# A message-passing network on one core: each tile's sums wait for the landing of a later piece's gather, and go tile by tile

## The chip, the cores and the metric

The kernel runs on one NeuronCore of a Trainium2 chip. The metric is the device time of one execution in microseconds (us); lower is better. Engines are named as in the profile: PE is TensorE (matmuls; PEld its weight loads), DVE is VectorE, ACT is ScalarE, POOL is GpSimd, which here issues the indirect DMAs, and SP is SyncE, which issues the plain ones.

## The reference

Four layers in a row act on x, 6250 nodes of 256 numbers; each is added to x after a layer normalisation. Cut to what matters here:

```
x = x + gat(layernorm(x), src, dst)            # layer 0: attention over 206250 edges, 4 heads of 64
x = x + moe(layernorm(x))                      # 8 experts, top 2
x = x + ngcf(layernorm(x), src, dst, weight)   # layer 1: weighted sums over the same 206250 edges
x = x + routed(layernorm(x), edge_index)       # 131072 more edges make the routing; 4 experts, top 2
```

The first is, for every node n and head, a softmax over the edges that end in n, and with it a sum over rows h[src]; the third is `segment_sum(weight * e[src], dst)`, then two dense products, a leaky ReLU and a division by the row's norm. Edges of the first and third come sorted by their target (`dst`); those of the fourth are sorted on the chip.

## The kernel before

An edge tile is 128 edges of the sorted list, and a piece is 8 tiles (`Q = 8`). A block is 128 nodes; there are 49. Because the edges are sorted, the tiles that can hold edges of block b form a window (`Stream.window`, L930), with a slack of 1024 edges on either side in the long lists and of 640 in the third. For one tile POOL gathers the 128 source rows from a table in DRAM by one indirect DMA; DVE makes a one-hot matrix for each block that the tile can touch (`one_hots`, L1056); and PE multiplies the one-hot matrix with the gathered rows into the block's accumulator in PSUM (the sums). An f32 matmul shows as two records, two passes, in the profile.

There are three such streams. The first two are the long ones: 1612 tiles, 202 pieces. Their order is written out by hand, within `tc.manual_schedule()`: every engine does its instructions in the order of the program text, and waits by semaphores for its operands and for its buffers.

*The first stream*, `gat_stream` (L1081) with `parts=1`, goes in steps. Step `s_` has:

- the gathers of piece `s_` (L1139) into one of 9 buffers; SP's loads for piece `s_ + 2`;
- for piece k = `s_ - 2`: the node products on PE (`node_parts`, L1160), the scores on DVE (`scores`, L1169 to L1175), and DVE's turned one-hots for the next piece (L1149);
- for piece q = `s_ - 7`: the sums of its tiles 0 and 1 (`sums(q, 0)`, L1239);
- in every fourth step a batch of 32 tiles: transposes on PE (`turn_scores`, L1185), two scans on DVE (`greatest`, L1191 to L1197);
- the one-hots for piece q + 1 (L1065); the sums of tiles 2 to 7 of piece q (`sums(q, 1)`); in a batch step the transposes back and the exponentials (`turn_back`, L1202 to L1210);
- the results of the blocks whose window has ended (`done`, L1650 to L1663), and DVE's product of messages for piece q + 1 (`messages`, L1217).

In a piece the sums go block by block, and within a block tile by tile.

*The second stream* (L1755 to L1795) has 6 buffers. Step `s_` gathers piece `s_` (L232, called in a helper), sums piece q = `s_ - 3` (L1780), does for ended blocks one stage each of a chain of functions (`side`, `dense`, `norm`, `next_ln`, `next_h`, `next_rows`; transposes on PE with copies on ACT, dense products, normalisations, and stores of the next layer's tables), and for piece k = `s_ - 2` scales the gathered rows by the edge weights on ACT (L1792) and makes the one-hots. A block's chain starts in the step after its last sum.

*The third stream* is `gat_stream` again with `parts=3`: the messages are split into three bf16 parts (L1222, L1224) and 787 tiles are summed by bf16 matmuls. Here `beside()` stands between the steps' parts: each call starts one unit of the last layer's feed-forward work, `inner` (L1533, four f32 passes of 512 columns) or `outer` (L1544, eight passes of 256), and finishes the unit before it by a gelu on ACT (L1538) or an addition on DVE (L1549).

Of the kernel before, what the change touches and what calls it, by code (L numbers as in the profile page):

```python
# [69 lines left out]
def tile_kernel(ctx, tc, src_ins, out):  # L70
    nc = tc.nc
# [157 lines left out]
        return v  # L229

    def gather(dst, table, si, t):
        nc.gpsimd.indirect_dma_start(  # L232
            out=dst, out_offset=None, in_=table,
            in_offset=bass.IndirectOffsetOnAxis(ap=si[:, t:t + 1], axis=0))


    def rstd_of(pool, var, n):
# [843 lines left out]
    def gat_stream(s, H, CD, si, il, dl, tab, NI, nid, early, done, parts=1, beside=None):  # L1081
# [6 lines left out]
        DH = H * CD  # L1088
# [3 lines left out]
        npiece = -(-T // Q)  # L1092
        PB = B // Q
        nbatch = -(-npiece // PB)
        with ExitStack() as st:
# [5 lines left out]
            with tc.tile_pool(name="split", bufs=1) as sp:  # L1101
                r = sp.tile([P, NT, ND], F32, name="r")
# [4 lines left out]
                nc.vector.tensor_copy(NB[:, :, 2, :], r)  # L1107
            ips = place_iota(pp)
            piece, Z, acc, turned, hots, dbs, kfs, ps, ended = {}, {}, {}, {}, {}, {}, {}, {}, []
            items, split = {}, {}  # L1110
            beside = beside or (lambda: False)

            def span(q):
                return q * Q, min(Q, T - q * Q)
# [10 lines left out]
            def load(q):  # L1125
                t0, n = span(q)
                dbs[q] = mp.tile([P, Q * P], I16, name="db", bufs=3)
                nc.sync.dma_start(dbs[q][:, :n * P], s.d16[t0 * P:(t0 + n) * P][None, :].to_broadcast([P, n * P]))
                if q % PB == 0:
                    i = q // PB  # L1130
                    kfs[i] = mp.tile([P, 3 * P + 1], BF, name="kf", bufs=3)
                    nc.sync.dma_start(kfs[i], bass.AP(tensor=s.keep.tensor, offset=s.keep.offset + i * B * P,
                                                      ap=[[P, B], [0, H], [1, 3 * P + 1]]))

            def gathers(q):
                t0, n = span(q)
                g = piece[q] = mp.tile([P, Q, W], F32, name="g", bufs=9)
                for j in range(n):
                    nc.gpsimd.indirect_dma_start(  # L1139
                        out=g[:, j, :DH + H], out_offset=None, in_=tab,  # L1140
                        in_offset=bass.IndirectOffsetOnAxis(ap=si[:, t0 + j:t0 + j + 1], axis=0))

            def turned_hots(q):
                t0, n = span(q)
# [83 lines left out]
            def sums(q, part):  # L1228
                t0, n = span(q)
                g = split[q]  # L1230
                for b, a, m, oh in hots[q]:
                    if b not in acc:
                        acc[b] = pp.tile([P, parts, W], F32, name="acc", bufs=2)
                        items[b] = early(b, mp)
                    lo, hi = s.window(b)
                    for t in range(a, a + m):
                        if (t - t0 < 2) == (part == 0):
                            m_ = g[:, t - t0, :] if parts == 1 else g[:, t - t0].rearrange("p s w -> p (s w)")
                            nc.tensor.matmul(acc[b].rearrange("p s w -> p (s w)"), oh[:, t - a], m_,  # L1239
                                             start=(t == lo), stop=(t == hi))  # L1240
                            if t == hi:
                                ended.append(b)
                if part == 1:
                    hots.pop(q)
                    split.pop(q, None)


            with tc.manual_schedule():
                load(0)
                load(1)  # L1250
                turned_hots(0)
                for s_ in range(max(npiece + 7, PB * nbatch + 3) + 1):
                    if s_ < npiece:
                        gathers(s_)
                    if s_ + 2 < npiece:
# [12 lines left out]
                    if batch:  # L1268
                        zt = turn_scores(i)
                        d, M = greatest(i, zt)  # L1270
                    if 0 <= q + 1 < npiece:
                        hots[q + 1] = one_hots(s, q + 1, mp, ips, dl, 4, F32 if parts == 1 else BF)
                    beside()
                    if 0 <= q < npiece:
                        sums(q, 1)
                    if batch:
                        turn_back(i, d, M)
                    beside()
                    while ended:
                        b = ended.pop(0)  # L1280
                        done(b, acc.pop(b), items.pop(b), mp)
                    if 0 <= q + 1 < npiece:
                        messages(q + 1)
                    beside()
                while beside():
                    pass
# [287 lines left out]
    def fast(flag_s0, last_d, dl_d):  # L1574
        s0 = flag_s0
# [102 lines left out]
        tab_e = dram.tile([NP, D], F32, name="tab_ef")  # L1678
# [3 lines left out]
        with tc.tile_pool(name="n1f", bufs=1) as ep, tc.tile_pool(name="n1fw", bufs=2) as mp, \  # L1682
# [14 lines left out]
                nc.sync.dma_start(tab_e[t0 * P:(t0 + n) * P].rearrange("(t p) d -> p t d", p=P), em[:, :n])  # L1697
            wg = layer1_weights(ep)
            ips = place_iota(pp)
            acc, piece, hots, ems = {}, {}, {}, {}  # L1700
            T = s0.T
            npiece = -(-T // Q)
            stages = {}

            def span(q):
                return q * Q, min(Q, T - q * Q)
# [50 lines left out]
            chain = {side: dense, dense: norm, norm: next_ln, next_ln: next_h, next_h: next_rows}  # L1757


            with tc.manual_schedule():  # L1760
                after = {}
                s_ = 0
                while s_ < npiece + 3 or any(k >= s_ for k in after):
                    if s_ < npiece:
                        t0, n = span(s_)
                        g = piece[s_] = mp.tile([P, Q, D], F32, name="g1", bufs=6)
                        for j in range(n):
                            gather(g[:, j, :], tab_e, si, t0 + j)
                    q = s_ - 3
                    if 0 <= q < npiece:  # L1770
                        t0, n = span(q)
                        g = piece.pop(q)
                        for b, a, m, oh in hots.pop(q):
                            lo, hi = s0.window(b)
                            if b not in acc:
                                acc[b] = pp.tile([P, D], F32, name="acc1", bufs=3)
                                ems[b] = mp.tile([P, D], F32, name="emb", bufs=3)
                                nc.sync.dma_start(ems[b], tab_e[b * P:(b + 1) * P])
                            for t in range(a, a + m):
                                nc.tensor.matmul(acc[b], oh[:, t - a], g[:, t - t0, :], start=(t == lo), stop=(t == hi))  # L1780
                            if hi == a + m - 1:
                                after.setdefault(s_ + 1, []).append((side, b, ()))
                    for f, b, args in after.pop(s_, []):
                        r = f(b, *args)
                        r = () if r is None else r if isinstance(r, tuple) else (r,)
                        if f in chain:
                            after.setdefault(s_ + 1, []).append((chain[f], b, r))
                    k = s_ - 2
                    if 0 <= k < npiece:
                        t0, n = span(k)  # L1790
                        for j in range(n):
                            nc.scalar.activation(piece[k][:, j, :], piece[k][:, j, :], AF.Copy,  # L1792
                                                 scale=wt[:, t0 + j:t0 + j + 1])
                        hots[k] = one_hots(s0, k, mp, ips, dl, 4)
                    s_ += 1  # L1795
# [19 lines left out]
    s0 = Stream("s0", I["src"].shape[0], SLACK0, N)  # L1815
# [32 lines left out]
```

## Time and profile before

| | |
|---|---|
| median of 3 runs | 6783.41 us (6782.30 to 6785.78) |
| the profiled execution | 6782.63 us, span of its instructions 6780.7 us |
| PE, DVE, ACT, POOL busy in the span | 5038.5, 3283.5, 1591.6, 4077.3 us |
| mean granted clock of PE | 0.845 |
| first stream, first to last gather's start | 183.0 to 2219.5 us (with the last one's end) |
| second stream | 3420.9 to 5437 us |
| third stream | 5457.2 to 6596 us |

The span is cut into 40 equal slices, and each digit is the busy share of a slice in tenths; PEclk is the clock that the throttle granted, in tenths of full speed:

```profile
PE   4477777777777669999577787877787727778778
PEld 3355555555555558888445555555555514445445
DVE  4466666666666781443422222222222246666663
ACT  2000000000000112322134444444444402222222
POOL 0677777777777012232167777777777767666650
PEclk9688888888888679999768888888888858889889
```

The two long stretches in which POOL stands at 7 are the first and the second stream; between them, where PE stands at 9, lies the mixture of experts. A busy POOL of 7 is the share of time in which a gather is being issued; what lies between two gathers is not counted.

### The profile page before, as it was taken

How to read it: one execution, taken by the hardware profiler on the slowest of the kernel's cores; microseconds unless marked ns; L12 is line 12 of the kernel's file. 1: busy time of each engine (PE TensorE's matmuls, PEld its weight loads, DVE VectorE, ACT ScalarE, POOL GpSimd, SP SyncE). 2: the span in 40 equal slices, each digit the busy share in tenths (PEclk: the TensorE clock that was granted, in tenths of full speed). 3: DMA queues.
4: the chain of work that ended last, by engine and by line, in shares of the span. 5: the costliest groups of instructions: out<-in, count | busy, mean ns of one | idle time of the engine just before them, and what ended most of it. 6: DMA issues, size and time to landing. Idle time of an engine off the chain costs nothing. (4 is left out here: it accounts for less than half of the span.)

```text
span 6780.7 us, 69471 instructions
## 1 busy us (share of the span) xinstructions
PE 5038.5 (74%) x23031; PEld 3781.3 (56%) x23031; DVE 3283.5 (48%) x7594; ACT 1591.6 (23%) x3641; POOL 4077.3 (60%) x4346
## 2 busy tenths in 40 slices
PE   4477777777777669999577787877787727778778
PEld 3355555555555558888445555555555514445445
DVE  4466666666666781443422222222222246666663
ACT  2000000000000112322134444444444402222222
POOL 0677777777777012232167777777777767666650
PEclk9688888888888679999768888888888858889889
DMA  4455555444555135557444343444433332222220
GB/s 138 137 138 138 139 136 138 137 138 135 140 138 136 46 107 194 181 190 237 144 121 112 112 113 111 113 113 112 112 112 112 112 84 42 43 44 37 42 42 12
DMA packets 462756, 777.63 MB, mean 115 GB/s; under 512 B 125744, under 2 KB 286928, under 8 KB 462355
## 3 DMA queue, kind: packets, MB, share of 16 engines
q0 software_dynamic: 190688, 461.74, 25.5%
q1 hardware_dynamic: 259166, 300.20, 14.6%
q10 hardware_dynamic: 12532, 11.16, 0.5%
q8 instruction: 185, 3.03, 0.2%
q14 instruction: 185, 1.51, 0.1%
HBM read 719.45 MB, written 56.48 MB: 114 GB/s over the span
## 5 line engine op out<-in xcount | busy, mean ns | idle before, releaser
L1139 POOL DMA_INDIRECT g<-tab,si x1612 | 1545.7, 959 | 603.1 <-issue 417.0
L232 POOL DMA_INDIRECT g<-tab_ef,si x1612 | 1525.2, 946 | 595.0 <-issue 566.6
L1780 PE MATMUL acc<-g,oh 128*128 128x256 f32 x4760 | 1421.7, 448 | 448.1 <-ACT g L1792 314.4
L1239 PE MATMUL acc<-g,oh 128*128 128x264 f32 x4760 | 1374.7, 454 | 432.5 <-issue 401.8
L1780 PEld LDWEIGHTS acc<-g,oh 128*128 128x128 f32 x4760 | 979.4, 219 | 863.8 <-ACT g L1792 700.8
L1239 PEld LDWEIGHTS acc<-g,oh 128*128 128x128 f32 x4760 | 1064.4, 229 | 656.3 <-issue 410.4
L1792 ACT ACTIVATE g<-g,wt 128x256 f32<-128x256 f32 x1612 | 797.3, 506 | 1007.9 <-DMA g<-tab_ef,si 1004.5
L1139 POOL DMA_INDIRECT g<-tab_1f,si1s x787 | 755.0, 959 | 403.9 <-issue 301.3
L1065 DVE TENSOR_TENSOR oh<-ips,dl 128x1024 f32<-128x1024 f32 (+6 forms) x680 | 712.0, 1080 | 54.3 <-PE acc L1780 53.1
L1533 PE MATMUL pf<-xt,w 128*128 128x512 f32 (+1 forms) x832 | 429.2, 655 | 112.1 <-DMA xt<-xt_df 71.2
L1724 DVE TENSOR_TENSOR on<-po,bias 128x256 f32<-128x256 f32 x49 | 20.8, 424 | 978.7 <-PE po L1722 978.7
L1217 DVE TENSOR_TENSOR g<-g,pe 128x2048 f32<-128x2048 f32 (+2 forms) x301 | 486.6, 1617 | 0.0
L1544 PE MATMUL pf<-w,h 128*128 128x256 f32 x1568 | 374.6, 389 | 43.8 <-DVE X L1549 43.6
L599 PE MATMUL ph<-xe,w 128*128 128x256 f32 x1792 | 400.6, 381 | 0.0
L612 PE MATMUL py<-w,h 128*128 128x256 f32 x1792 | 399.0, 381 | 0.0
L599 PEld LDWEIGHTS ph<-xe,w 128*128 128x128 f32 x1792 | 340.2, 191 | 44.7
L575 POOL DMA_INDIRECT xg<-tab_x,gi x112 | 123.7, 1104 | 397.2 <-PE pt L584 312.9
L612 PEld LDWEIGHTS py<-w,h 128*128 128x128 f32 x1792 | 337.7, 191 | 42.9
L1544 PEld LDWEIGHTS pf<-w,h 128*128 128x128 f32 x1568 | 290.3, 191 | 94.4 <-DVE X L1549 52.5
L1533 PEld LDWEIGHTS pf<-xt,w 128*128 128x128 f32 x832 | 162.6, 215 | 289.2 <-issue 144.6
L602 ACT ACTIVATE h<-ph,pa 128x256 f32<-128x256 f32 x448 | 211.9, 473 | 465.9 <-PE ph L599 465.5
L615 POOL DMA_INDIRECT tab_y<-y,so x112 | 118.2, 1055 | 264.1 <-DVE y L614 259.6
(453 smaller groups left out, 4432.3 us busy)
## 6 DMA issues: line engine op xcount, KB each, us to landing
w<-in_L_ffn_W SPq DMA_DIRECT2D x112, 1024.0 KB
db<-s_d SPq DMA_DIRECT2D x299, 256.0 KB
g<-tab,si POOLq DMA_INDIRECT x1612
g<-tab_ef,si POOLq DMA_INDIRECT x1612
g<-tab_1f,si1s POOLq DMA_INDIRECT x787
yy<-tab_y SPq DMA_DIRECT2D x7, 1792.0 KB
kf<-s_keep SPq DMA_DIRECT2D x76, 96.2 KB
bb<-in_L_ffn_b SPq DMA_DIRECT2D x56, 128.0 KB
```

Of the source, the lines that this page charges most:

```text
L232: nc.gpsimd.indirect_dma_start(out=dst, out_offset=None, in_=table, in_offset=bass.IndirectOffsetOnAxis(ap=si[:, t:t + 1], axis=0))
L599: nc.tensor.matmul(ph, w1[:, k, f * P:(f + 1) * P], xe[:, k, :], start=(k == 0), stop=(k == KD - 1))
L602: nc.scalar.activation(h, ph, AF.Gelu, bias=pa[:, f:f + 1])
L612: nc.tensor.matmul(py, hs[f][:, i * P:(i + 1) * P], w2[:, f, :], start=(f == 0), stop=(f == FC - 1))
L1065: nc.vector.tensor_tensor(o[:, :m], ips[:, None, k * P:(k + 1) * P].to_broadcast([P, m, P]), dl[:, a:a + m, None].to_broadcast([P, m, P]), ...
L1139: nc.gpsimd.indirect_dma_start(out=g[:, j, :DH + H], out_offset=None, in_=tab, in_offset=bass.IndirectOffsetOnAxis(ap=si[:, t0 + j:t0 + j ...
L1217: nc.vector.tensor_mul(gh, gh, ps[i][:, o:o + n, :, None].to_broadcast([P, n, H, CD]))
L1239: nc.tensor.matmul(acc[b].rearrange("p s w -> p (s w)"), oh[:, t - a], m_, start=(t == lo), stop=(t == hi))
L1533: nc.tensor.matmul(ph[:, :n], w1[:, e, k, f * P:(f + 1) * P], xts[g][:, k, :n], start=(k == 0), stop=(k == KD - 1))
L1544: nc.tensor.matmul(py[:, :D], hs[g, e, f][:, j * P:(j + 1) * P], w2[:, e, f, :], start=(f == 0), stop=(f == FC - 1))
L1780: nc.tensor.matmul(acc[b], oh[:, t - a], g[:, t - t0, :], start=(t == lo), stop=(t == hi))
L1792: nc.scalar.activation(piece[k][:, j, :], piece[k][:, j, :], AF.Copy, scale=wt[:, t0 + j:t0 + j + 1])
```

## The change

A matmul of the first stream that sums tile t of piece q gets one more dependency: on the landing of the gather of the same number in the piece that is being gathered in that step, q + 7 (the last gather of that piece if it has fewer). In the second stream it is the gather of piece `s_`, that is q + 3. The last pieces, for which no such piece exists, have none, and the third stream has none. In both streams of `gat_stream` and in the second stream the sums of a piece go tile by tile, and within a tile block by block. In `gat_stream`, and so in the third stream too, they are cut in three instead of two: tiles 0 and 1, tiles 2 to 4, and tiles 5 to 7; the last part stands behind the transposes back and one more call of `beside()`.

```
     def gather(dst, table, si, t):
-        nc.gpsimd.indirect_dma_start(
+        return nc.gpsimd.indirect_dma_start(
...
+    def after(inst, other):
+        tc.add_manual_dep(inst.ins, other.ins.name,
+                          mybir.DependencyInfo(mybir.DependencyClass.Sync, mybir.DependencyReason.DATA),
+                          reason="spread over the gathers' time")
...
-                for j in range(n):
-                    nc.gpsimd.indirect_dma_start(
-                        out=g[:, j, :DH + H], out_offset=None, in_=tab,
-                        in_offset=bass.IndirectOffsetOnAxis(ap=si[:, t0 + j:t0 + j + 1], axis=0))
+                came[q] = [gather(g[:, j, :DH + H], tab, si, t0 + j) for j in range(n)]
...
             def sums(q, part):
...
-                    lo, hi = s.window(b)
-                    for t in range(a, a + m):
-                        if (t - t0 < 2) == (part == 0):
+                for t in range(t0, t0 + n):
+                    for b, a, m, oh in hots[q]:
+                        lo, hi = s.window(b)
+                        if a <= t < a + m and (0 if t - t0 < 2 else 1 if t - t0 < 5 else 2) == part:
...
+                            mm = nc.tensor.matmul(acc[b].rearrange("p s w -> p (s w)"), oh[:, t - a], m_,
+                                                  start=(t == lo), stop=(t == hi))
+                            if spread and q + 7 < npiece:
+                                after(mm, came[q + 7][min(t - t0, len(came[q + 7]) - 1)])
...
                     if batch:
                         turn_back(i, d, M)
                     beside()
+                    if 0 <= q < npiece:
+                        sums(q, 2)
...
-                        for b, a, m, oh in hots.pop(q):
+                        bl = hots.pop(q)
+                        for b, a, m, oh in bl:
...
-                            for t in range(a, a + m):
-                                nc.tensor.matmul(acc[b], oh[:, t - a], g[:, t - t0, :], start=(t == lo), stop=(t == hi))
+                        for t in range(t0, t0 + n):
+                            for b, a, m, oh in bl:
+                                lo, hi = s0.window(b)
+                                if a <= t < a + m:
+                                    mm = nc.tensor.matmul(acc[b], oh[:, t - a], g[:, t - t0, :],
+                                                          start=(t == lo), stop=(t == hi))
+                                    if s_ < npiece:
+                                        after(mm, came[s_][min(t - t0, len(came[s_]) - 1)])
```

`spread` is `parts == 1`. The dictionary that was named `after` in the second stream is renamed `then`.

More of the change, by code (lines that the diff above doesn't have):

```diff
@@ L1109, in gat_stream @@
             piece, Z, acc, turned, hots, dbs, kfs, ps, ended = {}, {}, {}, {}, {}, {}, {}, {}, []
-            items, split = {}, {}
+            items, split, came = {}, {}, {}
             beside = beside or (lambda: False)
@@ L1230, in sums @@
                 g = split[q]
+                spread = parts == 1
                 for b, a, m, oh in hots[q]:
@@ L1234, in sums @@
                         items[b] = early(b, mp)
-                    lo, hi = s.window(b)
-                    for t in range(a, a + m):
-                        if (t - t0 < 2) == (part == 0):
+                for t in range(t0, t0 + n):
+                    for b, a, m, oh in hots[q]:
+                        lo, hi = s.window(b)
+                        if a <= t < a + m and (0 if t - t0 < 2 else 1 if t - t0 < 5 else 2) == part:
                             m_ = g[:, t - t0, :] if parts == 1 else g[:, t - t0].rearrange("p s w -> p (s w)")
-                            nc.tensor.matmul(acc[b].rearrange("p s w -> p (s w)"), oh[:, t - a], m_,
-                                             start=(t == lo), stop=(t == hi))
+                            mm = nc.tensor.matmul(acc[b].rearrange("p s w -> p (s w)"), oh[:, t - a], m_,
+                                                  start=(t == lo), stop=(t == hi))
+                            if spread and q + 7 < npiece:
+                                after(mm, came[q + 7][min(t - t0, len(came[q + 7]) - 1)])
                             if t == hi:
                                 ended.append(b)
-                if part == 1:
+                if part == 2:
                     hots.pop(q)
@@ L1699, in fast @@
             ips = place_iota(pp)
-            acc, piece, hots, ems = {}, {}, {}, {}
+            acc, piece, hots, ems, came = {}, {}, {}, {}, {}
             T = s0.T
@@ L1760, in fast @@
             with tc.manual_schedule():
-                after = {}
+                then = {}
                 s_ = 0
-                while s_ < npiece + 3 or any(k >= s_ for k in after):
+                while s_ < npiece + 3 or any(k >= s_ for k in then):
                     if s_ < npiece:
@@ L1766, in fast @@
                         g = piece[s_] = mp.tile([P, Q, D], F32, name="g1", bufs=6)
-                        for j in range(n):
-                            gather(g[:, j, :], tab_e, si, t0 + j)
+                        came[s_] = [gather(g[:, j, :], tab_e, si, t0 + j) for j in range(n)]
                     q = s_ - 3
@@ L1772, in fast @@
                         g = piece.pop(q)
-                        for b, a, m, oh in hots.pop(q):
-                            lo, hi = s0.window(b)
+                        bl = hots.pop(q)
+                        for b, a, m, oh in bl:
                             if b not in acc:
@@ L1778, in fast @@
                                 nc.sync.dma_start(ems[b], tab_e[b * P:(b + 1) * P])
-                            for t in range(a, a + m):
[L1780 to L1783, printed above, removed]
+                        for t in range(t0, t0 + n):
[6 more added lines that the diff above has]
+                                        after(mm, came[s_][min(t - t0, len(came[s_]) - 1)])
+                                    if t == hi:
+                                        then.setdefault(s_ + 1, []).append((side, b, ()))
+                    for f, b, args in then.pop(s_, []):
                         r = f(b, *args)
@@ L1786, in fast @@
                         if f in chain:
-                            after.setdefault(s_ + 1, []).append((chain[f], b, r))
+                            then.setdefault(s_ + 1, []).append((chain[f], b, r))
                     k = s_ - 2
```

## The prediction

> **What bounds the kernel now.** First the costliest groups of the page:
>
> ```profile
> L1139 POOL DMA_INDIRECT g<-tab,si x1612 | 1545.7, 959 | 603.1 <-issue 417.0
> L232 POOL DMA_INDIRECT g<-tab_ef,si x1612 | 1525.2, 946 | 595.0 <-issue 566.6
> L1780 PE MATMUL acc<-g,oh 128*128 128x256 f32 x4760 | 1421.7, 448 | 448.1 <-ACT g L1792 314.4
> L1239 PE MATMUL acc<-g,oh 128*128 128x264 f32 x4760 | 1374.7, 454 | 432.5 <-issue 401.8
> ```
>
> Both streams have 1612 gathers at about 0.95 us, each followed by idle time that nothing released. The waits of POOL, asked for from the first to the last gather of the first stream and then of the second, say how long the longest such pause is (columns: total, times, longest):
>
> ```profile
> POOL g L1139 <- issue: 417.0, 1369, 0.3
> ```
>
> ```profile
> POOL g L232 <- issue: 462.4, 1518, 0.3
> ```
>
> No pause inside either stream exceeds 0.3 us. A gather costs 0.945 + 0.305 = 1.25 us, a piece of eight 10.0 us, and 1612 of them 2015 us; the streams took 2036 (183.0 to 2219.5) and 2016 us (3420.9 to 5437). POOL is saturated in both. PE is busy 1430 of 2035 us in the first and 1612 of 2015 in the second, so it waits anyway. What is done to PE inside these streams can save nothing, and costs nothing until a gather finds its buffer still in use. What counts is the end of each stream: after the last gather, what PE still owes lies bare on the path. The timeline shows this for the first stream:
>
> ```profile
> 2194.63 6.84 PE L1239 MATMUL acc<-g,oh 128*128 128x264 f32 x30
> 2207.11 0.17 ACT L1650 ACTIVATE po<-acc 128x4 f32<-128x4 f32 x1
> 2216.40 0.19 DVE L1171 TENSOR_TENSOR z<-g,nd 128x32 f32<-128x32 f32 x1 [3.13 <-DMA g<-tab,si]
> 2218.51 0.95 POOL L1139 DMA_INDIRECT g<-tab,si  x1 [0.30 <-issue]
> ...
> 2227.75 20.69 PE L1239 MATMUL acc<-g,oh 128*128 128x264 f32 x80 [4.41 <-issue]
> ...
> 2266.63 0.42 DVE L1663 SCALAR_TENSOR_TENSOR X<-o,X 128x256 f32<-128x256 f32 x1
> ```
>
> (columns: start, duration, engine, line). The last gather starts at 2218.5, the last result stands at 2267.1: a drain of 47.6 us after POOL's end, and the next stage reads X. The second stream's end:
>
> ```profile
> 5435.97 0.95 POOL L232 DMA_INDIRECT g<-tab_ef,si  x1 [0.30 <-issue]
> ...
> 5438.50 1.98 PE L1780 MATMUL acc<-g,oh 128*128 128x256 f32 x8 [1.76 <-DVE oh L1065]
> 5439.22 0.51 ACT L1792 ACTIVATE g<-g,wt 128x256 f32<-128x256 f32 x1 [1.19 <-DMA g<-tab_ef,si]
> ...
> 5450.34 0.18 DVE L1753 COPY h<-ph 128x24 f32<-128x24 f32 x1 [2.21 <-PE ph L1748]
> ...
> 5457.23 0.94 POOL L1139 DMA_INDIRECT g<-tab_1f,si1s  x1 [20.32 <-DMA si1s<-si]
> ```
>
> Here ACT scales a tile as it lands (5439.22) and PE sums it right behind: at the last landing PE owes one piece, and 11 us later (5450.5) the stage is done. The third stream's POOL, idle 20.3 us, starts only after that.
>
> **The change, part by part.** *Steady state of the first two streams: 0.* The sums of piece q now wait, tile by tile, for the gathers of piece q+7 (first stream) or q+3 (second). No instruction is added, and DVE, ACT, POOL and SP keep their order; only PE's order and the counts it waits for change. Behind a waiting sum on PE stand the next step's node products and the transposes, and DVE's scores, the block results and ACT's copies wait for those. A tile's landing comes 2.9 us after its gather's start (the gather at 2213.51 released DVE at 2216.40), so a piece's last sum ends about 2.9 - 1.25 + 0.9 = 2.6 us after POOL has left piece q+7 (0.9: four passes of 0.23, the row 6.84/30). The first stream has 9 buffers, so POOL wants that buffer 10 us after that point: slack 7.4 us. The second has 6: slack 17 us. PE's need for a piece, 24 passes on average, is 24 x 0.23 = 5.5 us of 10. So POOL keeps its pace. Bounds: the longer gathers of the first stream (959 against 946 ns, 21 us in all) might vanish or double; DVE, whose work lies beside them, keeps all its instructions, so I take 0.
>
> *End of the first stream: +11.* The last piece (201) has four gathers, so tiles 3 to 7 of piece 194 all wait for the last landing, 2218.5 + 2.9 = 2221.4. Piece 194 has 15 products, 30 passes (the x30 counts); 18 of them come after that: 18 x 0.23 = 4.1, so 2225.5. Before, piece 194 was through by 2209.7. But before also stood still until piece 200 landed (2216.40), so not all of this is lost. Block 46 ends in tile 6, at 2225.0; its result and the product of DVE for the next piece take 4.9 us (2207.11 to 2213.0 less the 1.1 that DVE was still at other work): 2229.9. From the scores of piece 200 to the start of the 80 passes it took 2227.75 - 2216.40 = 11.3 us; now that begins at 2230.3, and the turn-back stands behind ten of the sixteen passes instead of all, which takes 2 us off: 2239.6 instead of 2227.75, +11.8; I take +11. From there both kernels have the same work. Bounds: if only PE's own lateness counts, 2225.5 - 2222.9 = +3; if nothing overlaps better, +14.
>
> *End of the second stream: +18.* At the last landing, 5439.2, PE now stands at tile 3 of piece 198, three pieces back. It owes 20 passes of that piece (two blocks), 16 + 16 + 8 of the next three. At 0.25 (another stretch: 60 passes in 14.9 us) piece 198 ends at 5444.2 and 199 at 5448.2. The transposes of block 47 and the row product of block 46 follow in PE's queue, 3.5 us as at 5424.67 to 5428.17: 5451.7. ACT, in order behind their copies, scales piece 200 (8 x 0.47) up to 5454.8, its sums end 5455.3, block 47's dense product (2.1) 5457.4, the last piece's 8 passes (2.0) 5459.4, against 5440.5: +18.9, of which I take 18. The tail behind it is as long as before. Bounds: bare passes alone, 52 x 0.23 = +12; the 60 passes at the pace of the first stream's slow sums (12 in 5.45, 0.45) 12 us more: +30.
>
> *Third stream: 0.* It has no new wait, but sums in three parts, and one unit of feed-forward work moves ahead of tiles 5 to 7:
>
> ```profile
> 6007.77 0.52 PE L1239 MATMUL acc<-s,oh 128*128 128x72 bf16 x11
> ...
> 6016.19 6.52 PE L1533 MATMUL pf<-xt,w 128*128 128x512 f32 x8
> ...
> 6022.88 1.96 PE L1533 MATMUL pf<-xt,w 128*128 128x512 f32 x4
> ```
>
> PE, DVE and ACT bind here: POOL's longest pause is 4.4 us. A unit is 2 us or more. Were a block's result to wait behind it, 49 blocks would pay up to 93 us. They don't: a block's window ends at tile 16b + 20, the fifth of its piece (the last block's at 786, the third), within the second part. It comes two small products later (0.047 each by the x11), 49 x 0.1 = 5 us at most; the turn-back and the unit come three to four earlier, 25 x 0.15 = 4 us at most. I take 0 between -4 and +5.
>
> *Sum.* 6782.6 (profiled execution: span 6780.7 and 1.9 around it) + 11 + 18 = 6811.6; the median stood 0.8 above that execution: **6812**. The terms' bounds give 6782.6 + 3 + 12 - 4 - 21 = 6773 to 6782.6 + 14 + 30 + 5 + 21 = 6853.
>
> The clock. The granted clock was 0.82 over the first stream and 0.85 over the second, and 1.00 from 4016 to 4032, where PE ran mostly two passes for each landing with pauses of about half a microsecond. So I expect spread sums to raise it, and the drains to begin at full speed; as POOL sets the pace, that buys nothing before them. The Trainium skill ("TensorE: Matmul & The Clock Gate", section "HAM oscillation — how this bites in real kernels") asks for no idle gaps over about 3.4 us and recommends bunching matmuls between DMA waits. Read as "bunch", it speaks against this change; read as "no long gap", for it. By the second reading the streams' time stays; by the first, a spread at half speed, the drains would be at their upper ends.
>
> **The rivals.** (1) *POOL stalls in the first stream.* A step with a batch and with a block's end puts scans, one-hots, turn-back, block result and DVE's product in a row behind node products that now start 2.6 us into the step. Counted from POOL's leaving piece q+6, by the rows: scores to 4.3, scans to 7.5, one-hots (2 x 1.2) to 9.8, turn-back to 11.6, result 14.3 to 15.2, product 17.5. The next piece's sums start 7.5 us into their step; 32 passes take 7.4 us at full speed (end at 15 of the 20 allowed) and 14.4 at 0.45 (22: a stall). Batches and block ends share a step for some nine blocks; 3 us each makes 27: 6839. With all 51 batches at 2 us, 6914. For it: the clock drops after PE's long waits. Against: a usual step needs 5.5 us of 10, so PE catches up 4.5 us in each.
>
> (2) *The third stream gives back more than the drains take: faster.* The place is its half-speed passes: L1533 ran at 0.82 a pass (6.52 for 8) or 0.49 (1.96 for 4; 0.43 in long rows, 6.87 for 16). Its 832 passes took 429 us; at 0.43 they need 358, so 71 us lie there. PE's groups follow closer on one another where the unit no longer waits for three tiles. It decides from 29 us (no loss) and is a measurable gain from 43, six tenths of all there is: 6812 - 71 = 6741 at best, and with two thirds of it 6765. For it: PE binds there. Against: the shift is 0.15 us, and the waits in between stay.
>
> (3) *It does not bite*: the earlier waits already held the sums as long, or the drains are hidden: 6783. Against it, PE's sums trail the landing by one tile in the second stream.
>
> **How the numbers follow.** Drains 0.66 (of it 0.59 slower by over 0.2%, 13.6 us, about what a measurement can tell from no change; 0.07 within); POOL stalls 0.14, slower; third stream 0.13 (0.08 faster, 0.04 within, 0.01 slower); no bite 0.07 (0.01 faster, 0.06 within). Faster 0.09, within 0.17, slower 0.74. The range is that of the sum's bounds, 6773 to 6853; it leaves out the larger gains (0.07) and the worst stalls (0.05).
>
> **What would show it.** Right: POOL's pauses in both streams still 0.3 us at the longest, the streams as long as before; the last product of the first stream some 59 us after POOL's last gather instead of 47.6, the second stream's last DVE copy some 32 us after its last gather's start instead of 14.4. Wrong: a POOL pause of microseconds at the first gather of a piece (rival 1), a shorter third stream with L1533 well below 429 us (rival 2), or drains as before (rival 3). My sum fails most easily in the drains, if the higher clock makes up for the pieces owed.

## The result and the profile after

The changed kernel took 6830.9 us (median of 4 runs, 6825.86 to 6835.65) beside 6783.18 us of the kernel before (4 runs): ratio 1.007, 95% interval 1.0052 to 1.0087. It is slower by 48 us where 29 us were forecast. Its profiled execution, the longest of the four, took 6835.65 us with a span of 6833.8, 53.1 us more than the span before.

The slices of the page, for PE, POOL and the granted clock:

```profile
PE   4477777777777669999558788778778827778778
...
POOL 0777777777777012232167777777777767666650
PEclk9688998888989679999767888887888858888889
```

In the first stream (slices 2 to 13) PEclk now shows more nines; POOL stands at 7 as before. The costliest groups of the page (busy time, mean ns of one, idle time before them and what ended most of it):

```profile
L232 POOL DMA_INDIRECT g<-tab,si x1612 | 1550.9, 962 | 603.9 <-issue 439.6
L232 POOL DMA_INDIRECT g<-tab_ef,si x1612 | 1526.7, 947 | 595.0 <-issue 553.3
L1245 PE MATMUL acc<-g,oh 128*128 128x264 f32 x4760 | 1451.6, 450 | 527.1 <-DMA g<-tab,si 358.5
L1792 PE MATMUL acc<-g,oh 128*128 128x256 f32 x4760 | 1423.6, 448 | 460.1 <-ACT g L1807 253.2
...
L1543 PE MATMUL pf<-xt,w 128*128 128x512 f32 (+1 forms) x832 | 436.8, 665 | 106.9 <-DMA xt<-xt_df 70.9
```

L1245 and L1792 are the sums, formerly L1239 and L1780. L1245's idle time is now ended by the landing of a gather (358.5 us), which is the added wait at work. The gathers of the first stream are 5.2 us longer in all (1545.7 before). L1543 (L1533 before) rose from 429.2 to 436.8 us. The waits of POOL inside the first stream, and inside the second (total, times, longest):

```profile
POOL g L232 <- issue: 439.6, 1443, 0.3
```

```profile
POOL g L232 <- issue: 449.0, 1474, 0.3
```

No pause of POOL exceeds 0.3 us, as before. So PE's new waits reach POOL nowhere inside a stream. The timeline at the end of the first stream (start, duration, engine, line; in brackets the idle time before it):

```profile
2224.30 0.95 POOL L232 DMA_INDIRECT g<-tab,si  x1 [0.30 <-issue]
...
2227.71 4.27 PE L1245 MATMUL acc<-g,oh 128*128 128x264 f32 x18 [0.70 <-DMA g<-tab,si]
...
2236.20 2.10 PE L1245 MATMUL acc<-g,oh 128*128 128x264 f32 x4 [4.03 <-DVE g L1221]
...
2246.44 3.80 PE L1245 MATMUL acc<-g,oh 128*128 128x264 f32 x16 [3.12 <-DVE g L1221]
...
2251.70 14.48 PE L1245 MATMUL acc<-g,oh 128*128 128x264 f32 x64 [1.46 <-DVE g L1221]
...
2288.36 0.14 POOL L1318 IOTA pid<- 128x1 int32 x1 [63.11 <-DVE X L1673]
```

The 18 passes at 2227.71 are tiles 3 to 7 of piece 194, released by the last landing. The 80 passes that began 9.2 us after the last gather's start now begin 22.1 us after it (2246.44). The last row reads the whole drain off POOL: it waits 63.1 us for the last X. Before, the same row was

```profile
2267.19 0.14 POOL L1308 IOTA pid<- 128x1 int32 x1 [47.73 <-DVE X L1663]
```

The end of the second stream, after the change:

```profile
5432.72 0.67 PE L1792 MATMUL acc<-g,oh 128*128 128x256 f32 x2 [0.55 <-DMA g<-tab_ef,si]
...
5455.92 17.10 PE L1792 MATMUL acc<-g,oh 128*128 128x256 f32 x78 [0.41 <-DVE ss L1743]
...
5461.10 0.94 POOL L232 DMA_INDIRECT g<-tab_ef,si  x1 [0.30 <-issue]
...
5475.97 3.70 PE L1792 MATMUL acc<-g,oh 128*128 128x256 f32 x16
...
5483.16 1.97 PE L1792 MATMUL acc<-g,oh 128*128 128x256 f32 x8 [1.76 <-ACT ss L1742]
...
5494.58 0.18 DVE L1763 COPY h<-ph 128x24 f32<-128x24 f32 x1 [2.35 <-PE ph L1758]
...
5502.39 0.94 POOL L232 DMA_INDIRECT g<-tab_1f,si1s  x1 [40.35 <-DMA si1s<-si]
```

The row at 5432.72 is what the change does in mid-stream: two passes for one landing, with a gap before them. When POOL starts its last gather PE still has most of a run of 78 passes before it, then 16, then 8. The last copy of h ends 33.7 us after the last gather's start, 14.6 before, and POOL waits 40.4 us for the third stream instead of 20.3.

Laid out by stretch (us; differences of starts and ends in the timelines of one profiled execution each; f1 to e6 are experiments below):

| | before | after | f1 order alone | f2 waits alone | f3 third as before | f4 ends free | e5 one less | e6 two less |
|---|---|---|---|---|---|---|---|---|
| first stream's gathers | 2036.4 | 2041.7 | 2033.3 | 2048.7 | 2040.7 | 2041.8 | 2038.8 | 2033.9 |
| its drain (last gather's end to last X) | 47.6 | 63.0 | 48.0 | 64.5 | 62.7 | 49.0 | 52.4 | 47.3 |
| experts, to the second stream's first gather | 1153.9 | 1156.5 | 1153.9 | 1155.8 | 1155.4 | 1156.0 | 1155.6 | 1154.9 |
| second stream's gathers | 2016.0 | 2017.3 | 2017.7 | 2018.6 | 2017.9 | 2018.3 | 2018.0 | 2021.2 |
| its drain (last gather's end to last h) | 13.6 | 32.7 | 14.0 | 35.4 | 32.8 | 13.6 | 26.5 | 23.0 |
| third stream's gathers | 1138.6 | 1146.5 | 1144.2 | 1140.3 | 1140.9 | 1143.7 | 1143.4 | 1145.5 |
| span | 6780.7 | 6833.8 | 6781.3 | 6838.3 | 6824.8 | 6795.5 | 6809.2 | 6800.3 |

Of the 53.1 us, 34.5 lie in the two drains, 7.9 in the third stream, 5.3 in the first stream, and 5.4 are spread over the rest.

### The profile page after: what moved, and what is told of

Same layout as the page of the kernel before. It is cut to its first block, busy times and chain, and to the rows that moved or that the text cites. A ratio compares the mean times of both kernels' runs of the same rounds, so it can differ in the third digit from the quotient of the medians.

```text
span 6833.8 us, 70856 instructions
## 1 busy us (share of the span) xinstructions
PE 5114.4 (75%) x23031; PEld 3686.9 (54%) x23031; DVE 3303.6 (48%) x7594; ACT 1463.2 (21%) x3641; POOL 4083.1 (60%) x4346
## 5 line engine op out<-in xcount | busy, mean ns | idle before, releaser
L232 POOL DMA_INDIRECT g<-tab,si x1612 | 1550.9, 962 | 603.9 <-issue 439.6
L1245 PE MATMUL acc<-g,oh 128*128 128x264 f32 x4760 | 1451.6, 450 | 527.1 <-DMA g<-tab,si 358.5
L1792 PE MATMUL acc<-g,oh 128*128 128x256 f32 x4760 | 1423.6, 448 | 460.1 <-ACT g L1807 253.2
L1792 PEld LDWEIGHTS acc<-g,oh 128*128 128x128 f32 x4760 | 985.9, 220 | 868.6 <-issue 409.7
L1245 PEld LDWEIGHTS acc<-g,oh 128*128 128x128 f32 x4760 | 952.8, 216 | 911.8 <-DMA g<-tab,si 580.0
L1807 ACT ACTIVATE g<-g,wt 128x256 f32<-128x256 f32 x1612 | 663.4, 495 | 52.8 <-DMA g<-tab_ef,si 51.9
L1734 DVE TENSOR_TENSOR on<-po,bias 128x256 f32<-128x256 f32 x49 | 20.8, 425 | 1087.2 <-PE po L1732 1087.2
L1543 PE MATMUL pf<-xt,w 128*128 128x512 f32 (+1 forms) x832 | 436.8, 665 | 106.9 <-DMA xt<-xt_df 70.9
L1173 DVE TENSOR_REDUCE nd<-pd 128x64 f32<-128x192 f32 (+1 forms) x301 | 106.7, 355 | 588.1 <-PE pd L1164 587.9
L1543 PEld LDWEIGHTS pf<-xt,w 128*128 128x128 f32 x832 | 165.0, 218 | 271.6 <-issue 154.0
```

The lines of the kernel that those rows point to most:

```text
L232: return nc.gpsimd.indirect_dma_start(out=dst, out_offset=None, in_=table, in_offset=bass.IndirectOffsetOnAxis(ap=si[:, t:t + 1], axis=0))
L1245: mm = nc.tensor.matmul(acc[b].rearrange("p s w -> p (s w)"), oh[:, t - a], m_, start=(t == lo), stop=(t == hi))
L1543: nc.tensor.matmul(ph[:, :n], w1[:, e, k, f * P:(f + 1) * P], xts[g][:, k, :n], start=(k == 0), stop=(k == KD - 1))
L1792: mm = nc.tensor.matmul(acc[b], oh[:, t - a], g[:, t - t0, :], start=(t == lo), stop=(t == hi))
```

## The experiments

The theory is that the waits make PE owe pieces at each stream's last landing, and that this debt lies bare in the drains. Its rivals are that the waits cost along the streams (longer gathers, late operands), and that the new order of the sums costs, in the third stream above all.

The four kernels whose labels begin e1 to e4 ran on a chip on which the kernel before itself takes 7972.89 us (27 runs, 7940.86 to 7992.89); the same four edits ran again as f1 to f4 on one where it takes 6781.77 us. The expectations of e1 to e4 were written in times of the second kind of chip, so what these four took can't be held against them. The drains of that chip don't settle the theory either: without the waits (e1) they are 64.2 and 47.6 us, with them (e3) 72.4 and 48.2, and the kernel before has no profile there. The argument rests on f1 to f4, e5 and e6.

**Order alone.** No sum has an added wait:

```
-                            if spread and q + 7 < npiece:
+                            if False:
...
-                                    if s_ < npiece:
+                                    if False:
```

> The changed kernel without its added waits: sums by tile and in three parts, nothing else. Theory (what PE owes at the last landing makes the loss): both drains as before, 47.6 us from the last gather's end to the last result in the first stream and 13.6 us in the second; what stays is the third stream's order, 1138.6 to 1146.4 us: 6783 + 8 = 6791 us. Rival A (the order by tile is the cost, by two accumulators in turn): 6820 to 6831, with long drains. Rival B (the third stream's order costs nothing, the 8 us were chance): 6783.

> The changed kernel without its added waits, on a chip where the kernel before takes its usual 6783 us. Theory (the loss is what PE owes at the last landing, the order itself costs little): both drains as before, 47.6 and 13.6 us; the third stream some 5 us longer, as in the runs with the sums tied to an earlier piece: 6788 us. Rival A (the order by tile is the cost in the first two streams): 6815 to 6831 and long drains.

e1 took 8018.57 us, 1.0057 [1.004, 1.0075] of before. f1 took 6784.99 us, 1.0003 [0.9994, 1.0012]: no difference, with drains of 48.0 and 14.0 us as before. So on f1's chip the new order by itself costs at most some 8 us, and the drains come from the waits.

**Waits alone.** The kernel before, block order and two parts, with the added waits:

```
                     for t in range(a, a + m):
                         if (t - t0 < 2) == (part == 0):
...
+                            if parts == 1 and q + 7 < npiece:
+                                after(mm, came[q + 7][min(t - t0, len(came[q + 7]) - 1)])
```

(and the same in the second stream).

> The kernel before with the added waits alone: sums by block, in two parts. Theory: the drains are those of the changed kernel or a few us longer, since a piece with two blocks has a whole block's tiles left behind its last landing (16 passes, 3.7 us, in place of 4): first stream +15 to +19, second +19 to +23, third stream 0: 6817 to 6826 us. Rival A (the order is the cost): 6783 to 6790.

> The kernel before with the added waits alone, by block and in two parts, on a usual chip. Theory: the drains of the changed kernel or up to 4 us more each (a second block's tiles stand behind the last landing): first stream +15 to +19, second +19 to +23, third 0: 6817 to 6826 us. Rival A: 6783 to 6790.

e2 took 7965.7 us, 0.9994 [0.9976, 1.0012]. f2 took 6834.23 us, 1.0076 [1.0062, 1.0089], the whole loss of the change, and 8 us above the upper end of what was expected. Its drains grew as expected (+16.9 and +21.8 us); its first stream's gathers took 12.3 us longer, which the expectation had left out. The end of its first stream in the timeline:

```profile
2230.77 0.94 POOL L232 DMA_INDIRECT g<-tab,si  x1 [0.30 <-issue]
...
2233.71 6.92 PE L1241 MATMUL acc<-g,oh 128*128 128x264 f32 x30
...
2296.35 0.14 POOL L1312 IOTA pid<- 128x1 int32 x1 [64.64 <-DVE X L1667]
```

Here 30 passes follow the last landing at a stretch, where the changed kernel had 18: in block order the early tiles of a part's second block stand behind the waiting late tiles of its first. Its waits of POOL also show pauses inside the first stream, which no other run on this chip has:

```profile
POOL g L232 <- issue: 454.1, 1471, 1.6
```

What its pauses have beyond 0.305 us comes to 6.5 us. The ten longer ones all stand ahead of the first gather of a piece, which is the sign that the prediction named for the stalls of rival (1). With the order by tiles the same waits cause none.

**Third stream as before**, the rest as changed: block order and two parts where `parts == 3`:

```
+                if parts == 3:
+                    order = [(t, *h) for h in hots[q] for t in range(t0, t0 + n)]
...
+                        w = 0 if t - t0 < 2 else 1 if t - t0 < 5 or parts == 3 else 2
...
-                    if 0 <= q < npiece:
+                    if 0 <= q < npiece and parts == 1:
                         sums(q, 2)
```

> The changed kernel with the third stream's sums as before (by block, two parts); the first two streams as changed. Theory: the third stream goes back from 1146 to 1139 us, the drains stay: 6831 - 8 = 6823 us. Rival B (the third stream's 8 us are chance, of the clock or of the run): 6831, and a third stream between 1139 and 1146 that doesn't follow the order.

> The changed kernel with the third stream's sums as before, on a usual chip. Theory: drains as in the changed kernel, the third stream back by 5 to 8 us to some 1139: 6824 us. Rival B (the third stream's loss is chance): 6831.

e3 took 7890.72 us, 0.9901 [0.9871, 0.9932]: faster there. f3 took 6826.57 us, 1.0065 [1.0051, 1.0079], which can't be told from the changed kernel's 1.007. Its third stream took 1140.9 us. Over the profiled executions, those with the new order there took 1143.4 to 1146.5 (after, f1, f4, e5, e6; mean 1144.7), those with the old 1138.6 to 1140.9 (before, f2, f3, and e8 below, 1140.1; mean 1140.0; e7, whose third stream is changed in another way, is left out). The new order costs some 4.7 us in the third stream.

What it changes there in every one of these executions is PE's time in the small bf16 sums themselves, before and after:

```profile
L1239 PE MATMUL acc<-s,oh 128*128 128x72 bf16 x1267 | 77.6, 209 | 93.4 <-DVE s L1222 93.4
```

```profile
L1245 PE MATMUL acc<-s,oh 128*128 128x72 bf16 x1267 | 91.6, 212 | 90.8 <-DVE s L1226 90.8
```

It is 77.5 to 77.6 us with the old order and 91.4 to 91.8 with the new one. How much of this makes up the 4.7 us was not measured.

**Ends free.** As changed, but a sum whose gather lies in the last eight pieces doesn't wait for it; the waits for gathers of the 194 pieces ahead of them stay:

```
-                            if spread and q + 7 < npiece:
+                            if spread and q + 7 < npiece - 8:
...
-                                    if s_ < npiece:
+                                    if s_ < npiece - 8:
```

> The changed kernel with the waits lifted from the sums whose gather lies in the last 8 pieces, so that PE can catch up before the streams end. Theory: both drains as before (47.6 and 13.6 us), the streams' pace as it was, the third stream's 8 us stay: 6791 us, though nearly all the waits (194 pieces of 202) are still there. Rival C (the waits cost along the whole stream, by longer gathers or by stalls): 6815 to 6831 us, with streams from first to last gather longer than 2036 and 2016 us by more than 5.

> The changed kernel with the waits lifted from the sums whose gather lies in the last 8 pieces, on a usual chip. Theory: with 194 of 202 pieces still waiting, both drains are as before; what stays is the third stream's 5 us and the up to 5 us by which the first stream's gathers were longer: 6788 to 6793 us. Rival C (the waits cost along the whole stream): 6815 to 6831.

e4 took 8005.4 us, 1.0038 [1.0023, 1.0053]. f4 took 6797.39 us, 1.0022 [1.0013, 1.0031], 4 us above the expected range and far from rival C. In its timeline, the end of the first stream and of the second:

```profile
2223.53 0.94 POOL L232 DMA_INDIRECT g<-tab,si  x1 [0.30 <-issue]
...
2236.86 14.48 PE L1245 MATMUL acc<-g,oh 128*128 128x264 f32 x64 [1.45 <-issue]
...
2273.59 0.14 POOL L1318 IOTA pid<- 128x1 int32 x1 [49.11 <-DVE X L1673]
```

```profile
5421.06 18.79 PE L1792 MATMUL acc<-g,oh 128*128 128x256 f32 x78 [0.37 <-DVE ss L1743]
...
5446.80 0.95 POOL L232 DMA_INDIRECT g<-tab_ef,si  x1 [0.30 <-issue]
...
5449.98 1.97 PE L1792 MATMUL acc<-g,oh 128*128 128x256 f32 x8 [1.76 <-DVE oh L1072]
...
5461.15 0.18 DVE L1763 COPY h<-ph 128x24 f32<-128x24 f32 x1 [2.10 <-PE ph L1758]
```

Eight pieces without waits bring both drains back, to 49.0 and 13.6 us. The run of 78 passes starts 25.7 us ahead of the last gather instead of 5.2. This settles the theory: 33.1 us of the loss in the profiled executions belong to the waits of the last pieces alone. It leaves 14.8 us in the span: 5.4 in the first stream, 5.1 in the third, 2.3 in the second, 2.1 between, 1.4 in the first drain, less 1.5 in the rest.

**One piece less, and two less.** The sums wait for q + 6 and q + 2, or for q + 5 and q + 1, instead of q + 7 and q + 3 (the first edit shown; the second has 5 and 1):

```
-                            if spread and q + 7 < npiece:
-                                after(mm, came[q + 7][min(t - t0, len(came[q + 7]) - 1)])
+                            if spread and q + 6 < npiece:
+                                after(mm, came[q + 6][min(t - t0, len(came[q + 6]) - 1)])
...
+                                    if q + 2 < npiece:
+                                        after(mm, came[q + 2][min(t - t0, len(came[q + 2]) - 1)])
```

> The changed kernel with each sum tied to the gather one piece earlier: q + 6 in the first stream, q + 2 in the second. Theory: one piece less is owed at each last landing. In the second stream that is 16 passes and no more than their turn in the queue, 4 to 6 us less than +19: +14. In the first, the sums of piece q then wait for the landing that the scores of the same step's end waited for before, so the drain is +0 to +5 instead of +15. Third stream +8: 6783 + 3 + 14 + 8 = 6808 us. Rival C (the waits cost by being there): 6831.

> The changed kernel with each sum tied to the gather two pieces earlier: q + 5 in the first stream, q + 1 in the second. Theory: the first stream's sums never came before that landing, so its drain is as before (+0); the second owes two pieces less than the changed kernel, +6 to +9 of the +19; third stream +8: 6783 + 0 + 8 + 8 = 6799 us. Rival C: 6831.

Beside a before of 6786.4 us, e5 took 6819.93 us, 1.0046 [1.0032, 1.006], and e6 6798.78 us, 1.0019 [1.001, 1.0028]; e6 is what was expected, e5 12 us more. e5's profiled execution was the shortest of its five, 9 us below their median, so its rows hold only part of that miss. The first drain, as POOL's wait in the timelines of e5 and then of e6:

```profile
2274.22 0.14 POOL L1318 IOTA pid<- 128x1 int32 x1 [52.50 <-DVE X L1673]
```

```profile
2265.10 0.14 POOL L1318 IOTA pid<- 128x1 int32 x1 [47.42 <-DVE X L1673]
```

With each piece that PE may be ahead the debt shrinks: 63.1, 52.5, 47.4 us, and by two pieces the first drain is that of before. In the second it goes 32.7, 26.5, 23.0 us and 14.0 without waits: there even one piece costs 9 us, because before PE summed a tile as soon as ACT had scaled it.

**The product for the next piece ahead of the block results.** An attempt on the first drain of the kernel before: DVE's product for piece q + 1 (`messages`) is issued ahead of the loop over `done`; in e7 in both streams of `gat_stream`, in e8 only where `parts == 1`:

```
+                    if 0 <= q + 1 < npiece:
+                        messages(q + 1)
                     while ended:
                         b = ended.pop(0)
                         done(b, acc.pop(b), items.pop(b), mp)
-                    if 0 <= q + 1 < npiece:
-                        messages(q + 1)
```

> The kernel before with one edit: in every step DVE makes the product of messages for the next piece ahead of the ended blocks' results. In the drains the next piece's sums waited for the product, which stood behind a block's result of 4 us; two such places lie in the first stream's drain. Theory: the first stream's drain shortens from 47.6 by 4 to 8 us, the saturated stretches stay; in the third stream, where PE waits for DVE's product, it gains up to 2 us in each of 49 block ends or loses as much on the results' gelu order: 6690 to 6790 us, 6775 taken. Rival (the drain is set by PE's passes alone): 6783 and a drain of 47 us.

> The same with the product ahead of the results in the first stream only; the third stream as before. Theory: the drain shortens by 4 to 8 us and nothing else moves: 6776 us. Rival (the drain is set by PE's passes alone): 6783.

e7 took 6790.2 us, 1.0004 [0.9995, 1.0013]; e8 6783.51 us, 0.9993 [0.9984, 1.0002]. The first drain of both is shorter by some 3 us (44.5 and 44.7 instead of 47.6), less than the 4 to 8 us expected, and the times can't be told from no change. No version tried here measurably beats the kernel before on the chips where it takes some 6783 us.

## Why the prediction was right, and where its sizes were off

*What bounds, and the steady state: right in kind.* POOL sets the pace of both streams, with no pause over 0.3 us before and after; PE's waits inside the streams reach nobody. The step's 0 was off by 5.3 us in the first stream, which is the gathers' own length (1550.9 against 1545.7 us). It lies within the 21 us set as its bound, and follows the wait: 1542.5 in f1 and 1542.9 in e6, 1548.0 in e5, and 1550.0 to 1551.6 in f2, f3 and f4. The trace shows where it lies, in a few gathers during which DVE makes a batch's difference `d` (L1197 before, L1201 after):

```profile
2034.12 1.36 POOL L232 DMA_INDIRECT g<-tab,si  x1 [0.31 <-issue]
...
2034.77 0.29 DVE L1201 TENSOR_TENSOR d<-zt,M 128x128 f32<-128x128 f32 x1
```

The stream has 49 such instructions of DVE. Before, 4 of them fell inside a gather, and these gathers took 1.07 us on the mean; after, 27 did, at 1.16 us. All other gathers stand at 0.959 us in both. It is 23 to 33 such gathers in f2 to f4 and e5, and 4, 1, 0 and 0 in f1, e6, e7 and e8. So the waits move DVE's batch work against the gathers; why a gather takes longer there stays open. The prediction's 5.5 us of PE per piece counted passes at 0.23 us; over the whole streams a pass took 0.29 and 0.30 (1374.7 and 1421.7 us by 4760), some 7 us of the 10, which still was enough.

*End of the first stream: +11 forecast, +15.4 measured, its upper bound +14.* The part up to the start of the last 80 passes was forecast at +11.8 and measured at +12.9; half of the difference is that the last landing released PE 3.4 us after its gather's start (2224.30 to 2227.71) and not 2.9. (The x30 row that the prediction shows at 2194.63 belongs to piece 193 and is cut by the view's start; the 30 passes of piece 194 and the 18 behind the landing are right all the same.) The term that was too small is "From there both kernels have the same work". In order by tiles the ending block's last sum stands among the last passes, and no longer ahead of the other block's, so its result comes behind the passes and not beside them: X ends 2.3 us after the 80 passes (2266.18 to 2268.49; 2.3 in f4 too), and 0.1 before (2248.44 to 2248.53), as these two rows of before and after show:

```profile
2248.11 0.42 DVE L1663 SCALAR_TENSOR_TENSOR X<-o,X 128x256 f32<-128x256 f32 x1
```

```profile
2268.07 0.42 DVE L1673 SCALAR_TENSOR_TENSOR X<-o,X 128x256 f32<-128x256 f32 x1
```

In f2, which has the old order, it is 0.1 too. The next 16 passes took 6.8 us from first to last instead of 4.1 (the first 4 in 2.10 instead of 1.13, behind 4.66 us in which PE stood idle instead of 2.39), of which 1.2 us reach the end. The hope that the drain would run at full speed held for its long run (64 passes in 14.48, 0.23 each; 80 in 20.69, 0.26 each, before), which gives back 0.95 us, but not for these. In sum, 12.9 + 2.2 + 1.2 - 0.95 = 15.35, the 15.4 measured.

*End of the second stream: +18 forecast, +19.1 measured.* The last 8 passes were forecast to end 18.9 us later against the last gather's start; they ended at 5485.13, 24.0 us after it, against 4.5: +19.5. The kind of debt named, three pieces with transposes and scalings in between, is what the timeline shows.

*Third stream: 0 forecast, bounds -4 and +5; +7.9 measured in the profiled execution*, and +4.7 between the means over five and four executions. The forecast weighed a unit ahead of the last tiles against earlier results and let the small sums keep their length; they took 91.6 us of PE instead of 77.6. Which of these costs the stream its time was not separated. The passes of L1543 took longer, not shorter.

*The sum.* 29 us forecast against 34.5 in the drains, and 13 more in the two streams to which 0 was given; the rest is small. The mechanism was right, the total short by 19 us in the median, and its largest misses are the two zeros, in the third stream and in the first stream's gathers. That the total lies within the range is owed to the wide bounds of the second drain and of the gathers: the first drain, and the third stream in this execution, lie above their own.

*The rivals.* The signs named for the sum came: POOL's pauses stayed at 0.3 us, and the drains were 63.0 us where 59 was named and 33.7 where 32 was. POOL stalls didn't appear in the changed kernel; they begin in f2, 6.5 us, where the waits meet the old order. The third stream gave nothing back: L1543 rose to 436.8 us instead of falling below 429.2. The waits bite, as L1245's 358.5 us of waiting for landings show.

*The clock.* Stretches inside the first and second stream of the kernel before (length; busy time of PE, PEld, DVE, ACT, POOL; granted clock, DMA share, GB/s):

```profile
184.00:2219.00 2035.00, 1429.64 (x7256) 1153.53 (x7257) 1305.88 (x2350) 78.07 (x393) 1544.23 (x1612) 0.82 0.51 138
3422.00:5437.00 2015.00, 1612.16 (x5610) 1129.73 (x5610) 485.49 (x853) 880.04 (x1941) 1524.24 (x1611) 0.85 0.40 112
```

The same of the changed kernel:

```profile
184.00:2219.00 2035.00, 1469.86 (x7181) 1035.60 (x7182) 1305.19 (x2329) 78.95 (x390) 1545.79 (x1607) 0.87 0.51 137
3422.00:5437.00 2015.00, 1582.33 (x5458) 1109.94 (x5458) 498.00 (x902) 729.81 (x1892) 1507.70 (x1592) 0.82 0.40 112
```

The same for the first stream of f1, order alone:

```profile
184.00:2219.00 2035.00, 1419.40 (x7270) 1136.07 (x7270) 1303.38 (x2355) 79.54 (x398) 1540.33 (x1610) 0.83 0.50 137
```

In the first stream the clock rose from 0.82 to 0.87. It takes the waits and the order together: order alone gave 0.83 (f1), waits alone 0.84 (f2). In the second it fell from 0.85 to 0.82, against the forecast, though the stretch from 4016 to 4032 on which the forecast rested lies in this stream. That the higher clock buys nothing where POOL sets the pace was right: the first stream is longer by 5 us. The Trainium skill ("TensorE: Matmul & The Clock Gate", section "HAM oscillation — how this bites in real kernels") names idle gaps of over about 3.4 us as what lowers the clock. In the first stream the traces agree: between its matmuls PE had 87 such gaps before, 75 in f1, 55 in f2 and 21 after. In the second stream it had none, before or after (the longest 2.4 and 2.3 us), and the clock fell all the same; what lowers it there was not found.

## What to carry to other kernels

A wait that holds work back to fill the gaps of a saturated feeder cost little here while the feeder ran (5 and 1 us in some 2000), and came due when it stopped: count what is owed at the last item and all that stands behind it in order, and let the last pieces go without the wait (f4 got 33 of 53 us back so). A raised clock on an engine that didn't set the pace was no gain. An order that changes which result comes last in a group can change the tail too, even where the number of instructions is the same (2.2 us here).

## What the runs showed of the hardware that was not expected

The same program took 17.5% longer on one chip (7972.89 against some 6783 us), and there POOL's gathers no longer run through. POOL's pauses in the first stream of e1, order alone, on that chip:

```profile
POOL g L232 <- issue: 784.2, 1496, 13.6
...
POOL g L232 <- PE acc L1245: 29.3, 17, 24.4
```

Against 0.3 us in f1, the same program on another chip, its gathers pause for up to 24.4 us here, and the stream takes 2477 us instead of 2033. Results of PE reach DVE late. In e1's second stream DVE's addition at L1734 follows PE's product at L1732:

```profile
4055.78 1.03 PE L1732 MATMUL po<-w,sT 128*128 128x256 f32 x4
...
4073.83 0.42 DVE L1734 TENSOR_TENSOR on<-po,bias 128x256 f32<-128x256 f32 x1 [31.34 <-remote]
```

It starts 17.0 us after the product's recorded end; in f1, the same program on the other chip, 0.04 us after it (3502.15 to 3502.19). Of the 49 such pairs, 42 are more than 5 us apart in e1, and none more than 0.04 us in f1. The stretch between the streams, where PE is dense, takes as long as on the other chips (1155.8 in e1, 1153.9 in f1). What makes the signals late was not found, and stays open.

On that chip the parts of the change also weigh differently. The new order in the third stream costs some 100 us (1535 and 1540 us in e1 and e4, 1439 and 1423 in e2 and e3). Waits and order in the long streams alone are faster than the kernel before there (e3, 0.9901 [0.9871, 0.9932]), while the waits without the order are not (e2). Taken from e1 and e3, it is the order more than the waits: without the some 100 us of the third stream, order alone would stand some 50 us under the kernel before, where order and waits stand 82 under it. This is a subtraction and not a run, and without a profile of the kernel before on that chip it isn't shown where the gain lies.
